# The columns W a of three attention layers: from VectorE to TensorE

## Chip, cores and metric

The kernel runs on one core of a Trainium2 chip. The metric is the device time of one execution in microseconds (us). Each line number below is one of the kernel before.

## What is computed

Four graph attention layers follow one another on x (16 graphs of 1024 nodes with 256 features), all with one 0/1 adjacency matrix. Each layer normalises x per node, applies relu, and adds the layer's result to x. Layers 1 and 3 have 4 heads of 64 columns, layers 2 and 4 one head of 256. In short:

```python
h = relu(layernorm(x))
Wh = h @ W                                   # (N, H * D)
e = leaky(Wh @ a_src + (Wh @ a_dst).T)       # per head, N x N
x = x + act(softmax(where(adj, e, -inf)) @ Wh)   # elu; relu in the last layer
```

Since `Wh @ a = h @ (W @ a)`, the kernel holds for each layer a tile `wx` with the columns of W and, beside them, the columns W a_dst and W a_src of each head. One projection of h by `wx` then gives Wh and both scores. This case is about how the extra columns are made, once per layer.

## The kernel before

**Tiling.** A graph's 1024 nodes lie on 128 partitions as C = 8 blocks, its 256 features as K = 2 halves. Graphs run in four streams, and a step `n` is one layer of one graph; there are 64 steps, in the order that `order_of_steps` writes out (the first steps are layer 1 of graphs 0, 1 and 2, layer 2 of graph 0, and so on).

**A step's work.** A step is prepared while earlier steps are aggregated. VectorE takes statistics (`stats`, L243), GpSimd or VectorE turns them into scale and shift (`combine`, `combine_end`, L272 to L284; all GpSimd in the steps that matter here), ScalarE normalises (L290) and splits the floats into 16-bit halves (L299), a DMA from SyncE's queue transposes them (L301), and ScalarE merges them (L307). TensorE projects (`project`, L332), ScalarE evacuates the result (L334) and takes exponentials (L340, L342), and GpSimd scales (L344). `factors` and `rows` write one row of factors per head to DRAM (L350 to L362), from where SyncE loads it spread over all partitions (`fetch`, L386) and ScalarE copies it to PSUM (`broadcast`, L397). Then VectorE makes the weights, one 128 x 1024 tile for each head and block of neighbours (`weights`, L411, one instruction each). TensorE sums weights times Wh in eight groups per step (`aggregate`, L428): with four heads a group is half a head (64 matmuls, 128 instructions), with one head a block of nodes (8 matmuls, 16 instructions). ScalarE evacuates each group (L443), and `finish` (L464 to L493) divides, applies the activation and adds to x.

**Order.** The program is written out by hand: under `manual_schedule` each engine executes its instructions in the order in which the code issues them. The loop at the end goes through steps and groups; after group k of step n it calls what `later[8 * n + k]` holds, then what `prepare` finds due, then emits more weight tiles.

**Buffers.** The tiles named `w` share 18 slots (`WBUFS`). The weight tiles use them, at first the adjacency rows too, and so do the vectors of `weight_columns`. A tile that finds no free slot waits until an earlier one was read for the last time. PSUM banks named `bank` are four.

**The columns.** `weight_columns(l)` returns four pieces. `vectors` loads a (2 KB) to one partition by one DMA on SyncE's queue (L145). `spread` copies it to all partitions by a matmul with ones (L152) and a ScalarE copy (L155). `columns` makes, for each k and each of the two vectors, a product (L162) and a sum along the row (L163) on VectorE, and the squares of one column set (L169). `bound` sums the squares by TensorE (L175) and derives the layer's constants (L178 to L182). Layer 1 does this at the start. The three other layers do it during the run:

```python
for l, at in ((1, 1), (2, 8 * 3 + 3), (3, 8 * 5 + 3)):
    for i, piece in zip((0, 1, 2, 8), layer[l]):
        later[at + i] = piece
```

So the four pieces follow groups 1, 2, 3 and 9, counted from 0, for the second layer (l = 1), groups 3, 4, 5 and 11 counted from 0 at step 3 for the third (l = 2), and the same from step 5 for the fourth (l = 3).

Of the kernel before, what the change touches and what calls it, by code (L numbers as in the profile page):

```python
# [26 lines left out]
F32 = mybir.dt.float32  # L27
# [4 lines left out]
AF = mybir.ActivationFunctionType  # L32
ALU = mybir.AluOpType
# [3 lines left out]
P = 128  # L37
# [3 lines left out]
WBUFS = 18  # L41
# [29 lines left out]
def kernel(ctx: ExitStack, tc: tile.TileContext, x, adj, ws, avs, out):  # L71
    nc = tc.nc
    B, N, F = x.shape
    C = N // P
    K = F // P
# [4 lines left out]
    ident = const.tile([P, P], F32, name="ident")  # L80
# [10 lines left out]
    wx = []  # L91
# [12 lines left out]
    small = ctx.enter_context(tc.tile_pool(name="small", bufs=4))  # L104
    work = ctx.enter_context(tc.tile_pool(name="work", bufs=2))
# [10 lines left out]
    def bank(*shape):  # L116
        t = ps.tile([P, 512], F32, name="bank")
        n = math.prod(shape)
        if len(shape) == 1:
            return t[:, 0:n]  # L120
        names = "abc"[:len(shape)]
        return t[:, 0:n].rearrange(f"p ({' '.join(names)}) -> p {' '.join(names)}",
                                   **dict(zip(names, shape)))

    def heads_of(t, H):


        return t[..., 0:F + H].rearrange("p c (h d) -> p c h d", h=H)
# [6 lines left out]

    def weight_columns(l):

        H, slope, hs, _ = LAYERS[l]
        D = F // H
        st = {}  # L140

        def vectors(queue=nc.sync):

            st["a"] = work.tile([P, HALF, H, D], F32, name="w", bufs=WBUFS)
            queue.dma_start(  # L145
                out=st["a"][0:1, 2:4],
                in_=bass.AP(tensor=avs[l].tensor, offset=avs[l].offset,
                            ap=[[0, 1], [D, 2], [hs, H], [1, D]]))

        def spread():  # L150
            pa = bank(2, H, D)
            nc.tensor.matmul(pa.rearrange("p t h d -> p (t h d)"), lhsT=ones[0:1, :],  # L152
                             rhs=st["a"][0:1, 2:4].rearrange("p t h d -> p (t h d)"),
                             start=True, stop=True)
            nc.scalar.activation(st["a"][:, 0:2], pa, AF.Copy)  # L155

        def columns(ks=range(K)):
            for k in ks:
                for part in range(2):
                    prod = st["a"][:, 2 + part]  # L160
                    wk = heads_of(wx[l], H)[:, k]
                    nc.vector.tensor_mul(prod, wk[:, :, 0:D], st["a"][:, part])  # L162
                    nc.vector.tensor_reduce(  # L163
                        wk[:, :, D] if part else wx[l][:, k, F + H:F + 2 * H], prod, AX.X, ALU.add)
            if K - 1 not in ks:
                return
            st["sq"] = small.tile([P, K, H], F32, name="sq", bufs=1)
            wd = heads_of(wx[l], H)[:, :, :, D]
            nc.vector.tensor_tensor(st["sq"], wd, wd, op=ALU.mult)  # L169

        def bound():

            pn = bank(H)
            for k in range(K):
                nc.tensor.matmul(pn, lhsT=ones, rhs=st["sq"][:, k, :], start=(k == 0),  # L175
                                 stop=(k == K - 1))
            top = small.tile([P, 1], F32, name="top", bufs=1)
            nc.vector.tensor_reduce(top, pn, AX.X, ALU.max)  # L178
            nc.gpsimd.tensor_tensor(top, top, half1, op=ALU.pow)
            nc.gpsimd.tensor_scalar(cbias[l], top, 16.01, None, op0=ALU.mult)  # L180
            nc.gpsimd.tensor_scalar(nbias[l], top, -16.01 * slope, None, op0=ALU.mult)
            nc.gpsimd.tensor_scalar(rbias[l], top, -16.01 * (1.0 - slope), SHIFT,  # L182
                                    op0=ALU.mult, op1=ALU.add)

        return vectors, spread, columns, bound

    pairs = {}
# [413 lines left out]
    for n, (b, l) in enumerate(steps):  # L601
# [6 lines left out]
        start = 8 * (n - 2)  # L608
# [5 lines left out]
        if free > start + kind[0]:  # L614
            kind = LATE
            start = max(free, agenda_of[-1][0] + 5, start - LATE[7])
        if n == len(steps) - 1:
            kind, start = LAST, 8 * (n - 1)
# [8 lines left out]
    with tc.manual_schedule():  # L627
        blocks = [mask_rows(c) for c in range(C)]
        layer = [weight_columns(l) for l in range(L)]
        layer[0][0](nc.scalar)  # L630
        load(0, 2)
# [100 lines left out]
```

## Time and profile before

| what | value |
|---|---|
| median of 4 runs | 2449.03 us (2447.83 to 2451.18) |
| the profiled execution | 2448.02 us, span 2446.2 us |
| TensorE matmuls busy | 2393.2 us (98% of the span) |
| VectorE busy | 2049.0 us (84%) |
| ScalarE busy | 1478.4 us (60%) |
| GpSimd busy | 1072.7 us (44%) |
| mean granted TensorE clock | 0.996 |
| L162, four layers | 16 instructions, 8.1 us |
| L163, four layers | 16 instructions, 6.7 us |

In the profile PE is TensorE (PEld its weight loads), DVE VectorE, ACT ScalarE, POOL GpSimd and SP SyncE; SPq is SyncE's queue, from which DMAs are issued. A line of the timeline gives the start and the duration in us, engine, line and operation, what is written and read, how many instructions were merged, and in brackets the engine's idle time before it with what ended it. A float32 matmul appears as two instructions. The chain is the sequence of work and waits that ended last, followed back from the end. The granted clock is TensorE's, as a share of full speed.

### The profile page before, as it was taken

The numbers are of one execution on the slowest core, as the hardware profiler recorded it, in microseconds if no ns is written. First come the engines' busy times: TensorE is split into PE (matmuls) and PEld (weight loads), VectorE is DVE, ScalarE is ACT, GpSimd is POOL, SyncE is SP. The second block draws the span as 40 slices with busy tenths as digits, with TensorE's granted clock in tenths as the row PEclk, the third lists the DMA queues.
The fourth block names the chain that finished last, engine by engine and source line by source line (L and its number), as shares of the span: only waits on it lengthen the run. The fifth ranks groups of instructions, "written<-read, shape, count | busy, mean of one in ns | idle before, by whom it ended". The sixth has DMA issues, their size and how long they took to land.

```text
span 2446.2 us, 86561 instructions
## 1 busy us (share of the span) xinstructions
PE 2393.2 (98%) x39127; PEld 2149.3 (88%) x39127; DVE 2049.0 (84%) x2168; ACT 1478.4 (60%) x2499; POOL 1072.7 (44%) x1346
## 2 busy tenths in 40 slices
PE   7999999999999999999999999999999999999999
PEld 5888798889898899898898888999988998988897
DVE  8988688988878988888888889888889888889794
ACT  5464676556665656765556665566665567656542
POOL 3345455443345454544433554543443445554331
PEclk9999999999999999999999999999999999999999
DMA  4322232233333322333333322223324323323310
GB/s 182 81 54 63 44 80 60 73 98 92 101 74 94 80 63 46 80 71 96 107 95 89 80 62 71 63 56 104 83 85 113 97 46 79 69 64 80 71 54 35
DMA packets 290442, 191.84 MB, mean 78 GB/s; under 512 B 259998, under 2 KB 262806, under 8 KB 288152
## 3 DMA queue, kind: packets, MB, share of 16 engines
q1 hardware_dynamic: 290062, 186.29, 30.0%
q8 instruction: 307, 5.03, 0.8%
q14 instruction: 63, 0.52, 0.1%
q10 hardware_dynamic: 10, 0.00, 0.0%
HBM read 104.87 MB, written 17.43 MB: 50 GB/s over the span
## 4 chain that ended last, share of the span: by engine, by line
PE 80%; ACT 7%; DVE 5%; DMA 4%; issue 2%; POOL 1%; SPq 0%; DVEq 0%; ACTq 0%
PE bank L428 62%; PE bank L332 18%; DVE w L411 3%; ACT rows L290 2%; DMA gs<-grow 2%; DMA grow<-gT 2%; ACT rows L299 1%; ACT g L397 1%; ACT rows L481 1%; DMA rows<-rows 1%; ACT y L443 1%; ACT rows L307 1%; DVE bn L243 1%; DVE rows L487 0%; PE bank L358 0%
## 5 line engine op out<-in xcount | busy, mean ns | idle before, releaser
L428 PE MATMUL bank<-whx,w 128*64 128x65 f32 x36864 | 1896.4, 240 | 15.8 <-DVE w L411 9.7
L428 PEld LDWEIGHTS bank<-whx,w 128*64 128x64 f32 x36864 | 1745.5, 144 | 173.1 <-ACT whx L334 21.5
L411 DVE SCALAR_TENSOR_TENSOR w<-g,rcol,mask 128x1024 f32<-128x1024 f32 (+1 forms) x1288 | 1539.6, 1267 | 193.2 <-PE bank L428 162.6
L344 POOL TENSOR_TENSOR whx<-whx 128x1024 f32<-128x1024 f32 x128 | 245.4, 1917 | 840.7 <-ACT whx L342 840.7
L443 ACT ACTIVATE y<-bank 128x260 f32<-128x260 f32 (+1 forms) x504 | 191.7, 381 | 560.5 <-PE bank L428 560.4
L332 PE MATMUL bank<-wx,rows 128*128 128x264 f32 (+1 forms) x2048 | 485.5, 391 | 14.2 <-ACT y L443 6.5
L332 PEld LDWEIGHTS bank<-wx,rows 128*128 128x128 f32 x2048 | 381.4, 191 | 90.1 <-ACT rows L307 12.8
L475 POOL TENSOR_TENSOR y<-y,r 128x1024 f32<-128x1024 f32 x124 | 257.8, 2088 | 224.5 <-DVE rows L474 188.7
L334 ACT ACTIVATE whx<-bank 128x264 f32<-128x264 f32 (+1 forms) x512 | 193.8, 388 | 190.2 <-PE bank L332 189.8
L290 ACT ACTIVATE rows<-x,shift,rstd 128x256 f32<-128x256 f32 x512 | 264.5, 588 | 67.4 <-POOL shift L284 62.3
L488 POOL TENSOR_TENSOR x<-x,rows 128x1024 f32<-128x1024 f32 x94 | 222.3, 2365 | 177.9 <-DVE rows L487 177.9
L307 ACT ACTIVATE rows<-rows 128x2048 uint16<-128x2048 uint16 x122 | 261.7, 2145 | 20.4 <-DMA rows<-rows 20.3
L299 ACT ACTIVATE rows<-rows 128x2048 uint16<-128x2048 uint16 x122 | 233.2, 1911 | 3.9
L487 DVE SCALAR_TENSOR_TENSOR rows<-rows,y 128x1024 f32<-128x1024 f32 x94 | 185.9, 1978 | 45.0 <-ACT rows L481 39.5
L243 DVE BATCH_NORM_STATS2 bn<-x 128x6 f32<-128x256 f32 x512 | 175.8, 410 | 34.4 <-POOL x L488 31.1
L397 ACT ACTIVATE g<-gs 128x1024 f32<-128x1024 f32 x158 | 161.6, 1023 | 63.6 <-DMA gs<-grow 48.7
L278 POOL TENSOR_TENSOR rstd<-rstd,neghalf 128x4 f32<-128x4 f32 (+1 forms) x97 | 121.3, 1251 | 41.1 <-DVE shift L279 33.8
L481 ACT ACTIVATE rows<-rows 128x1024 f32<-128x1024 f32 x96 | 100.6, 1048 | 9.9 <-DVE rows L510 7.9
L464 DVE RECIPROCAL r<-y 128x32 f32<-128x32 f32 (+1 forms) x63 | 17.3, 275 | 98.5 <-ACT y L443 98.5
L474 DVE SCALAR_TENSOR_TENSOR rows<-y,r 128x1024 f32<-128x1024 f32 x58 | 68.5, 1222 | 1.1
L342 ACT ACTIVATE whx<-whx,nbias 128x16 f32<-128x16 f32 (+1 forms) x128 | 40.2, 314 | 4.2
L340 ACT ACTIVATE rcol<-whx,rbias 128x16 f32<-128x16 f32 (+1 forms) x128 | 39.9, 312 | 4.2
(73 smaller groups left out, 465.6 us busy)
## 6 DMA issues: line engine op xcount, KB each, us to landing
gs<-grow SPq DMA_DIRECT2D x158, 512.0 KB
x<-in_x SPq DMA_DIRECT2D x15, 1024.0 KB
out<-x SPq DMA_DIRECT2D x30, 512.0 KB
w<-in_adj SPq DMA_DIRECT2D x8, 512.0 KB
rows<-rows SPq DMA_TRANSPOSE x122
x<-in_x SPq DMA_DIRECT2D x2, 512.0 KB
wx<-in_L_gnn_W SPq DMA_DIRECT2D x8, 128.0 KB
out<-x SPq DMA_DIRECT2D x8, 128.0 KB
```

The lines of the kernel that those rows point to most:

```text
L243: nc.vector.bn_stats(bn[:, c, :], xs[b][:, c, :])
L290: nc.scalar.activation(xn[:, :, q, :], xs[b][:, c, :].rearrange("p (k i) -> p k i", k=K), AF.Relu, bias=st["shift"][:, c:c + 1], scale=st[ ...
L299: nc.scalar.activation(bits, xn.rearrange("p (n s) -> p s n", s=2), AF.Copy)
L307: nc.scalar.activation(st["hT", half].rearrange("p k i -> p (k i)").bitcast(U16).rearrange("p (n s) -> p n s", s=2), st["turned", half].re ...
L332: nc.tensor.matmul(pw, lhsT=st["hT", half][:, k, q * P:(q + 1) * P], rhs=wx[l][:, k, :], start=(k == 0), stop=(k == K - 1))
L334: nc.scalar.activation(st["whx"][:, c, :], pw, AF.Copy)
L344: nc.gpsimd.tensor_tensor(wh[:, :, :, 0:D], wh[:, :, :, 0:D], wh[:, :, :, D:D + 1].to_broadcast([P, HALF, H, D]), op=ALU.mult)
L411: nc.vector.scalar_tensor_tensor(state[n]["w", h, j][:, s], state[n]["g", h][:, s], state[n]["rcol"][:, j, h:h + 1], masks[LAYERS[steps[n] ...
L428: nc.tensor.matmul(acc[o % P:o % P + cols, q, :], lhsT=st["w", h, jc][:, o:o + cols], rhs=st["whx"][:, jc, h * (D + 1):(h + 1) * (D + 1)], ...
L443: nc.scalar.activation(st["y"][:, i0:i0 + per, h, :], acc, AF.Copy)
L475: nc.gpsimd.tensor_tensor(yh, yh, rb, op=ALU.mult)
L488: nc.gpsimd.tensor_add(xh, xh, e)
```

## The change

For the second, third and fourth layer, three of the four pieces are replaced; layer 1 keeps the old ones, `bound` stays, and the places in `later` are the same.

- `vectors_down` lays the vectors down the partitions, one element per partition, in a tile with a column for each vector and head. For four heads the tile is first zeroed on GpSimd, and eight DMAs of 64 elements each follow; for one head there are four DMAs of 128 elements and no zeroing. All are on SyncE's queue.
- `turned` transposes W by matmuls with the identity (four of 128 x 128 for one head, eight of 64 x 128 for four heads) and copies the result to a second tile named `w` on ScalarE.
- `products` multiplies W by the vectors in four small matmuls. Two ScalarE copies bring the columns into `wx`, and GpSimd squares one set.

VectorE no longer takes part in these layers, except for the maximum in `bound`.

```diff
+        def vectors_down():
+            a = st["a"] = work.tile([P, K, 2 * H], F32, name="w", bufs=WBUFS)
+            if H > 1:
+                nc.gpsimd.memset(a, 0.0)
+            for part, column in ((1, 0), (0, H)):
+                for h in range(H):
+                    for k in range(K):
+                        if h * D // P <= k <= ((h + 1) * D - 1) // P:
+                            lo = max(h * D, k * P)
+                            size = min((h + 1) * D, (k + 1) * P) - lo
+                            nc.sync.dma_start(
+                                out=a[lo - k * P:lo - k * P + size, k, column + h:column + h + 1],
+                                in_=bass.AP(tensor=avs[l].tensor,
+                                            offset=avs[l].offset + h * hs + part * D + lo - h * D,
+                                            ap=[[1, size], [1, 1]]))
+        def turned():
+            pt = bank(K, K, P)
+            for k in range(K):
+                wk = heads_of(wx[l], H)[:, k, :, 0:D]
+                size = min(D, P)
+                for lo in range(0, F, size):
+                    h, d = divmod(lo, D)
+                    nc.tensor.matmul(pt[lo % P:lo % P + size, lo // P, k, :],
+                                     lhsT=wk[:, h, d:d + size], rhs=ident, start=True, stop=True)
+            st["wT"] = work.tile([P, K, K, P], F32, name="w", bufs=WBUFS)
+            nc.scalar.activation(st["wT"], pt, AF.Copy)
+        def products():
+            pw = bank(K, 2 * H)
+            for k in range(K):
+                for d in range(K):
+                    nc.tensor.matmul(pw[:, k, :], lhsT=st["wT"][:, d, k, :], rhs=st["a"][:, d, :],
+                                     start=(d == 0), stop=(d == K - 1))
+            wd = heads_of(wx[l], H)[:, :, :, D]
+            nc.scalar.activation(wd, pw[:, :, 0:H], AF.Copy)
+            nc.scalar.activation(wx[l][:, :, F + H:F + 2 * H], pw[:, :, H:2 * H], AF.Copy)
+            st["sq"] = small.tile([P, K, H], F32, name="sq", bufs=1)
+            nc.gpsimd.tensor_tensor(st["sq"], wd, wd, op=ALU.mult)
+        if l > 0:
+            return vectors_down, turned, products, bound
         return vectors, spread, columns, bound
```

## The prediction

> **What bounds the kernel now.** First the page: the busy shares, then the chain that ended last.
>
> ```profile
> PE 2393.2 (98%) x39127; PEld 2149.3 (88%) x39127; DVE 2049.0 (84%) x2168; ACT 1478.4 (60%) x2499; POOL 1072.7 (44%) x1346
> ...
> PE 80%; ACT 7%; DVE 5%; DMA 4%; issue 2%; POOL 1%; SPq 0%; DVEq 0%; ACTq 0%
> ```
>
> TensorE idles 53 of 2446.2 us and carries 80% of the chain, so an edit counts where it lengthens or shortens TensorE's idle time. DVE, which the change relieves, carries 5%. All edits lie before 335 us: the second layer's pieces at 45 to 106 us, the third's at 200 to 240, the fourth's at 283 to 328. What the three places are bound by, the timeline, the chain in order of time and the busy times by stretch must tell.
>
> ```profile
> 62.02 1.12 PE L152 MATMUL bank<-w,ones 1*128 1x512 f32 x2
> ...
> 73.36 26.30 DVE L411 SCALAR_TENSOR_TENSOR w<-g,rcol,mask 128x1024 f32<-128x1024 f32 x22
> ...
> 87.03 3.95 PE L428 MATMUL bank<-whx,w 128*64 128x65 f32 x128
> ...
> 112.14 7.50 PE L428 MATMUL bank<-whx,w 128*64 128x65 f32 x244 [0.86 <-DVE w L411]
> ```
>
> Second layer (timeline): DVE is busy without a gap from 45 to 150 us, and between 109 and 136 TensorE waits for it in nine pieces, some 7 us. Here DVE is the bound.
>
> ```profile
> 200.17 2.79 DMA w<-in_L_gnn_a
> 202.95 0.14 issue
> 203.09 1.09 PE bank L152 x2
> 204.18 10.62 PE bank L428 x48
> 214.80 3.49 PE bank L332 x16
> ...
> 283.74 1.54 DMA w<-in_L_gnn_a
> 285.28 0.14 issue
> 285.41 1.09 PE bank L152 x2
> ```
>
> Third and fourth layer (the chain in order of time): TensorE itself is on the chain, and waits 1.27 and 1.18 us for the vector's DMA before the old spread matmul. A transfer that comes late here is paid in full.
>
> ```profile
> 204.84 0.23 POOL L284 TENSOR_SCALAR shift<-shift 128x4 f32<-128x4 f32 x1
> ...
> 228.97 7.24 DVE L411 SCALAR_TENSOR_TENSOR w<-g,rcol,mask 128x1024 f32<-128x1024 f32 x6 [5.83 <-PE bank L428]
> ```
>
> ```profile
> 249.00:255.00 6.00, 4.74 (x82) 4.55 (x84) 5.99 (x12) 5.97 (x7) 3.31 (x11) 0.50 0.71 137
> ```
>
> For the third layer the timeline adds that GpSimd works on statistics until 205.07, and that DVE later stands 5.8 us for TensorE, so DVE is not the bound there. The row below it is of the busy times by stretch: six microseconds, the busy time and instructions of PE, PEld, DVE, ACT and POOL, then the granted clock, 0.50 after a run of waits.
>
> **Second layer, L162 to L169 gone from DVE.** Nine instructions from 70.02 to 73.36: 3.3 us of the bounding engine. Not all arrives. The 22 products that follow are 1.195 us each; the 17th (it begins at 92.48) is tile 42 in the kernel's count from 0, and needs the slot of tile 24, for there are 18 slots. TensorE last reads tile 24 in the last quarter of the group at 87.03, at about 87.03 + 3.0 + 0.1 = 90.1. TensorE is itself delayed: two small ScalarE copies come ahead of the merge L307, which releases the projection at 71.95; the nearest rows (L340, 0.30) make 0.6. So DVE gains 92.5 - 90.1 - 0.6 = **1.8 us**, which TensorE gets where it waits at 109 to 136. Ends: 3.3 if the slot is free earlier, a loss of 0.6 if DVE turns out not to bind. The vectors' four DMAs (issued from 45.6) have 20 us before they are used; SyncE's next work is at 63.85. The turning (four matmuls, eight instructions; L394 did eight of 128x128 in 1.04) takes the place of the spread (1.12).
>
> **Third layer.** Here the step is moved in the queues, so each is followed.
> - Before, SyncE issued the vector at 200.17. Now the tile is first zeroed on GpSimd, which has both halves' statistics (L272 to L284) ahead in its order, until 205.07. A memset of 128x8 took 0.10, so SyncE starts at 205.2.
> - It then issues eight DMAs of 64 single elements. Back to back, the eight L195 took 4.74, or 0.59 each; the shortest issue rows of SyncE are 0.33, the longest L133 0.69. The last starts seven issues later: 205.2 + 4.1 = 209.3 (207.5 to 210.0). From issue to landing the vector took 1.54 with the rings empty and 2.79 behind a 512 KB load; I take 1.5, as nothing is ahead: **210.8** (209.0 to 212.8).
> - TensorE is free at 201.82 and need not wait for the vectors to turn W: eight logical matmuls, 16 instructions, 1.0 us if column halves overlap as at L428, 2.1 if they do not. The sixth of the step's eight groups follows (10.62 / 3 = 3.54), so it reaches the products at 206.4 to 207.5, say **206.9**, and stands **3.9 us**.
> - The products are eight instructions; L175, four in 0.5 to 0.6, makes 1.1. End 211.9. Before, the same group ended at 204.18 + 3.54 = 207.7. Loss **4.2 us** (2.4 to 6.2).
> - Nothing downstream hides it: the seventh and eighth group, and the projection at 214.64, are TensorE's own chain, and DVE at 228.97 starts when TensorE frees its tiles. The 3.3 us taken from DVE at 208.91 are worth nothing here. With vectors and turned W both held, eight tiles in use and eight ahead fill the 18 slots, so the ninth product ahead must wait until TensorE has done the column products: DVE idles where it did the columns. Behind SyncE's eight issues stands the first transpose (205.72, now about 210); its merge ended 2 us before TensorE's need of 214.64, which itself moves by more than 4. Cost nothing, as the stall covers it; without that cover, some 2 us.
>
> **The clock.** After the waits of 246 to 250 us the granted clock fell to 0.50, and the 228 instructions from 250.75 took 8.83 where 384 at full clock took 11.42: 228 x 0.0297 = 6.8, so 2.0 lost. At 118 to 122 it fell although TensorE was busy 2.30 of 4.00 us, and stayed low for some 6.5. A stall of 3.9 is emptier than either stretch, so I count a fall, with the last two groups under it: 5 us at half rate, **2.5 us** (0 to 3.4). The Trainium skill ("TensorE: Matmul & The Clock Gate", Part 1, the HAM clock gate) has the clock halved after at least one idle window of about 3.4 us and back after one busy window. By that rule a stall of 3.9 would fill a whole window only by luck of phase, and cost about 1.7, an estimate from the page; the row at 118 to 122 speaks for an earlier fall, and the measurement decides.
>
> **Fourth layer.** No memset (one head). Four DMAs in place of one at 283.74; the last lands by 283.74 + 3 x 0.59 + 1.5 = 287.0 (up to 288.6), before the products at 288.9. TensorE saves the wait (1.18), pays turning for spread and 1.1 for the products: about -0.2. But the row of factors (L362, 284.19) and its broadcast (L386) are issued behind, 0.9 to 1.9 us later, and ScalarE's copy of it (L397, 289.07) stands ahead of the evacuations that TensorE's third projection needs; that gives back 0 to 1.5. Together **+0.3** (-1.5 to +1.2). DVE's 4.7 us there lie in idle time: its tiles were ready at 304.5, used at 307.67.
>
> The square on GpSimd, the bound's matmuls L175 and the other copies have tens of microseconds of cover. The Trainium skill ("DMA: Bandwidth & Descriptors", Rules for kernel authors) speaks against the change: a last dimension that isn't contiguous becomes one descriptor per element, to be avoided. No row before shows such a load, so the sum keeps the rows above.
>
> **Sum.** -1.8 + 4.2 + 2.5 + 0.3 = **+5.2 us**. The profiled execution took 2448.02 (span 2446.2 and 1.8 around it), so 2453.2; the median of the runs is 2449.03, 1.0 above, so **2454.2**. The ends: -3.3 + 2.4 + 0 - 1.5 = -2.4, and 0.6 + 6.2 + 3.4 + 1.2 = +11.4.
>
> **Rivals.**
> 1. *The stall stays short of the clock.* Same path, no fall: -1.8 + 2.4 to 4.2 + 0.3, about 2450 to 2452. For it: short waits near 136 and 151 left the clock at 1.00.
> 2. *Not slower: the vectors land before TensorE gets to the products.* It decides at 206.9. Then the third layer is -1.27 - 1.12 + 1.0 + 1.1 = -0.3, the fourth at its best -1.5, and the second up to -3.3: 2444, or 2445.5 with the second at -1.8. Against it: GpSimd ends its statistics at 205.07, which leaves 1.7 us for eight issues and a landing.
> 3. *Element loads are slow to issue.* If each takes a transpose's median on SyncE (1.93), the last starts at 218.7 and lands at 220.2: stall 13, with the clock about +16, or 2465. Against it: every plain SyncE load is 0.26 to 0.69.
>
> That the change does not relieve DVE is no rival; that DVE then waits in place of working is in the sum.
>
> **How the numbers follow.** About 0.2% (4.9 us) is what a measurement of this kernel can tell from no change. The forecast has 0.55, of which its range puts 0.43 above that bound and 0.12 within. Rival 1 has 0.20 (within), rival 2 0.14 (0.09 faster, 0.05 within), rival 3 0.11 (slower). So slower 0.54, within 0.37, faster 0.09. The range 2446.5 to 2460.5 spans the two ends and leaves out rival 3 and the better part of rival 2. The likeliest case alone spans 2452 to 2460.5.
>
> **What would show it.** Right: in the third layer the last vector DMA issues after GpSimd's L284 and TensorE shows a gap of some 4 us on the vectors' DMA ahead of the products, then a clock near 0.50; in the second, TensorE's waits on L411 shrink from 7 to about 5 us; in the fourth, no wait on the vectors. Wrong: products that start at once in the third layer (rival 2), or issue rows above 1 us (rival 3), or time that appears past 335 us, of which this sum has none.

## The result, and the profile after

The changed kernel's median is 2454.74 us (2448.88 to 2463.43), against 2450.63 us of the kernel before, run on the same chips. The ratio is 1.002 with a 95% interval of 1.0014 to 1.0026, which is 3.4 to 6.4 us and at its middle 4.9 us: slower, by about as much as this measurement can tell at all. (The ratio is an estimate of its own and not the quotient of the medians, which are 4.1 us apart.) Two executions on the chip of runs 9 to 11, at 3476.57 and 5638.01 us, were in a slower state and are left out of all ratios and medians below. The profiled execution took 2455.11 us, its span is 2453.3 us.

First the page of the changed kernel: the busy shares and the chain by engine.

```profile
PE 2399.0 (98%) x39177; PEld 2157.9 (88%) x39177; DVE 2038.2 (83%) x2141; ACT 1481.9 (60%) x2505; POOL 1072.5 (44%) x1350
...
PE 85%; ACT 6%; DVE 3%; DMA 3%; issue 2%; POOL 1%; SPq 0%; DVEq 0%; ACTq 0%
```

DVE lost 10.8 us of work, and the span grew by 7.1. TensorE's idle time hardly moved (53.0 before, 2453.3 - 2399.0 = 54.3 now), its busy time grew by 5.8. So the page alone says that no wait took over on the whole, and that TensorE works longer. Both are sums over places that moved in opposite directions; the places have to be read one by one.

A ruler for that is the time at which TensorE starts three projections, in each profile's timeline: one after the second layer's DVE-bound stretch (140.39 us before), one after the third layer's pieces (214.64), one after the fourth's (332.44). What a profile adds between two marks is what that layer cost. A caution: the marks of a kernel are those of one execution, and before 59 us, where TensorE's work is still the same, the executions already differ by -1.4 to +0.3 us; the changed kernel's profile is 0.8 early there (its "early start" below).

| mark | before | after | difference | added by the layer |
|---|---|---|---|---|
| second layer done | 140.39 | 136.59 | -3.80 | -3.0 (0.8 is the early start) |
| third layer done | 214.64 | 220.18 | +5.54 | +9.34 |
| fourth layer done | 332.44 | 338.09 | +5.65 | +0.11 |

**Second layer.** In the timeline (start, duration, engine, line, operation, and in brackets the idle time ahead and what ended it) the kernel before has this at the projection's third block:

```profile
80.64 1.03 ACT L397 ACTIVATE g<-gs 128x1024 f32<-128x1024 f32 x1 [2.32 <-DVE w L411]
82.87 2.13 ACT L307 ACTIVATE rows<-rows 128x2048 uint16<-128x2048 uint16 x1
85.05 2.05 PE L332 MATMUL bank<-wx,rows 128*128 128x264 f32 x8 [1.26 <-ACT rows L307]
```

and the changed kernel this (L455 is the old L411, L441 the old L397, L351 the old L307, L376 the old L332, L472 the old L428):

```profile
48.08 47.75 DVE L455 SCALAR_TENSOR_TENSOR w<-g,rcol,mask 128x1024 f32<-128x1024 f32 x40
...
77.57 1.02 ACT L441 ACTIVATE g<-gs 128x1024 f32<-128x1024 f32 x1
80.27 2.14 ACT L351 ACTIVATE rows<-rows 128x2048 uint16<-128x2048 uint16 x1
83.03 2.05 PE L376 MATMUL bank<-wx,rows 128*128 128x264 f32 x8
...
85.00 3.95 PE L472 MATMUL bank<-whx,w 128*64 128x65 f32 x128
```

Before, ScalarE's copy of the factors waited 2.32 us until DVE had read the previous ones, the merge stood behind that copy, and TensorE behind the merge. With the nine DVE instructions gone, ScalarE no longer waits, nor TensorE, which is here 2.0 us earlier, of which 0.8 is the early start. DVE makes 40 tiles from 48.08 to 95.83 without a gap.

**Third layer.** The timeline of the changed kernel (L328 is the old L284):

```profile
201.02 0.23 POOL L328 TENSOR_SCALAR shift<-shift 128x4 f32<-128x4 f32 x1
201.19 0.11 POOL L190 MEMSET w<- 128x16 f32 x1
201.33 5.55 SPq L197 DMA_DIRECT2D w<-in_L_gnn_a  x8
...
207.64 0.56 PE L219 MATMUL bank<-w 128*128 128x8 f32 x2 [4.92 <-DMA w<-in_L_gnn_a]
208.89 1.42 PE L219 MATMUL bank<-w 128*128 128x8 f32 x6 [0.68 <-DMA w<-in_L_gnn_a]
210.16 10.18 PE L472 MATMUL bank<-whx,w 128*128 128x257 f32 x32
210.50 2.48 DVE L455 SCALAR_TENSOR_TENSOR w<-g,rcol,mask 128x1024 f32<-128x1024 f32 x2 [6.50 <-PE bank L219]
```

The memset follows the last statistics instruction of GpSimd, SyncE's eight issues follow the memset, and TensorE stands 4.92 and 0.68 us for their data. The two groups behind the products take 10.18 us, where three took 10.69 before. The chain in order of time gives the landing of the last vector, and the busy times by stretch (PE, PEld, DVE, ACT, POOL, then the granted clock) the clock over the two groups:

```profile
206.28 2.36 DMA w<-in_L_gnn_a
```

```profile
206.00:216.00 10.00, 7.68 (x22) 6.44 (x23) 2.48 (x2) 3.16 (x5) 0.20 (x1) 0.50 0.57 106
```

**Fourth layer.** Timeline of the changed kernel:

```profile
288.06 2.75 SPq L197 DMA_DIRECT2D w<-in_L_gnn_a  x4
...
290.91 0.29 SPq L406 DMA_DIRECT2D grow<-gT  x1
...
294.11 0.95 PE L219 MATMUL bank<-w 128*128 128x2 f32 x8
...
295.95 1.03 ACT L441 ACTIVATE g<-gs 128x1024 f32<-128x1024 f32 x1 [2.49 <-DMA gs<-grow]
...
297.18 0.17 ACT L222 ACTIVATE wx<-bank 128x2 f32<-128x2 f32 x1
...
297.34 5.61 PE L376 MATMUL bank<-wx,rows 128*128 128x264 f32 x24 [0.40 <-ACT wx L222]
```

No wait for the vectors is left; a small new one stands at the column copy L222, of which more below.

### The profile page after: what moved, and what is told of

The parts are those of the page before. It is cut to its first block, busy times and chain, and to the rows that moved or that the text cites. A ratio compares the mean times of both kernels' runs of the same rounds, so it can differ in the third digit from the quotient of the medians.

```text
span 2453.3 us, 86699 instructions
## 1 busy us (share of the span) xinstructions
PE 2399.0 (98%) x39177; PEld 2157.9 (88%) x39177; DVE 2038.2 (83%) x2141; ACT 1481.9 (60%) x2505; POOL 1072.5 (44%) x1350
## 3 DMA queue, kind: packets, MB, share of 16 engines
q8 instruction: 307, 5.03, 0.8%
## 4 chain that ended last, share of the span: by engine, by line
PE 85%; ACT 6%; DVE 3%; DMA 3%; issue 2%; POOL 1%; SPq 0%; DVEq 0%; ACTq 0%
PE bank L472 66%; PE bank L376 18%; ACT rows L334 2%; DVE w L455 2%; DMA gs<-grow 1%; DMA grow<-gT 1%; ACT rows L343 1%; ACT rows L351 1%; ACT g L441 1%; ACT rows L525 1%; DVE rows L531 1%; DVE bn L287 0%; ACT y L487 0%; DMA rows<-rows 0%; PE bank L402 0%
## 5 line engine op out<-in xcount | busy, mean ns | idle before, releaser
L472 PE MATMUL bank<-whx,w 128*64 128x65 f32 x36864 | 1901.6, 241 | 17.7 <-DVE w L455 8.5
L472 PEld LDWEIGHTS bank<-whx,w 128*64 128x64 f32 x36864 | 1749.3, 144 | 174.4 <-ACT whx L378 22.2
L455 DVE SCALAR_TENSOR_TENSOR w<-g,rcol,mask 128x1024 f32<-128x1024 f32 (+1 forms) x1288 | 1540.0, 1270 | 208.9 <-PE bank L472 168.2
L376 PE MATMUL bank<-wx,rows 128*128 128x264 f32 (+1 forms) x2048 | 484.1, 390 | 11.2 <-ACT y L487 7.2
L376 PEld LDWEIGHTS bank<-wx,rows 128*128 128x128 f32 x2048 | 381.2, 190 | 85.8 <-ACT y L487 11.5
L351 ACT ACTIVATE rows<-rows 128x2048 uint16<-128x2048 uint16 x122 | 261.5, 2144 | 25.2 <-DMA rows<-rows 25.2
L441 ACT ACTIVATE g<-gs 128x1024 f32<-128x1024 f32 x158 | 162.0, 1025 | 58.7 <-DMA gs<-grow 49.7
```

Source lines behind the costliest of these rows:

```text
L351: nc.scalar.activation(st["hT", half].rearrange("p k i -> p (k i)").bitcast(U16).rearrange("p (n s) -> p n s", s=2), st["turned", half].re ...
L376: nc.tensor.matmul(pw, lhsT=st["hT", half][:, k, q * P:(q + 1) * P], rhs=wx[l][:, k, :], start=(k == 0), stop=(k == K - 1))
L455: nc.vector.scalar_tensor_tensor(state[n]["w", h, j][:, s], state[n]["g", h][:, s], state[n]["rcol"][:, j, h:h + 1], masks[LAYERS[steps[n] ...
L472: nc.tensor.matmul(acc[o % P:o % P + cols, q, :], lhsT=st["w", h, jc][:, o:o + cols], rhs=st["whx"][:, jc, h * (D + 1):(h + 1) * (D + 1)], ...
```

## The experiments

What the profile suggests is one theory with two halves: **the second layer gains because DVE, its bound, has less to do; the third loses because its vectors are late (their memset stands behind GpSimd's statistics, and eight issues behind the memset) and because the stall brings the clock down.** The rivals: that the pieces cost TensorE in the third layer by their own work or by holding slots of `w`, whenever the vectors come; that the gain of the second layer is not DVE's; and that something beyond 335 us gives or takes. Each run is given by the three marks and by the time against the kernel before:

| run | second | third | fourth | third layer alone | median against before, us | ratio (95%) |
|---|---|---|---|---|---|---|
| the change | -3.80 | +5.54 | +5.65 | +9.34 | 2454.74 / 2450.63 | 1.0020 (1.0014 to 1.0026) |
| e1_third_only | +0.11 | +8.04 | +7.76 | +7.93 | 2459.23 / 2447.68 | 1.0043 (1.0028 to 1.0057) |
| e2_second_fourth | -3.19 | -1.69 | -1.59 | +1.50 | 2447.58 / 2447.68 | 1.0000 (0.9988 to 1.0013) |
| e3_zero_early | -3.15 | -2.74 | -3.31 | +0.41 | 2449.27 / 2447.68 | 1.0001 (0.9987 to 1.0015) |
| e4_products_later | -3.52 | +0.35 | +0.20 | +3.87 | 2449.34 / 2447.68 | 1.0008 (0.9996 to 1.0020) |
| e5_filled | -3.97 | +1.52 | +1.97 | +5.49 | 2455.33 / 2450.46 | 1.0024 (1.0011 to 1.0038) |
| e6_four_dmas | -4.13 | +2.12 | +2.26 | +6.25 | 2453.99 / 2450.46 | 1.0008 (0.9994 to 1.0022) |
| e7_dve_kept | +0.35 | +8.17 | +7.78 | +7.82 | 2460.77 / 2450.46 | 1.0031 (1.0020 to 1.0042) |
| e8_vectors_early | -3.47 | -3.74 | -3.66 | -0.27 | 2450.71 / 2450.46 | 0.9991 (0.9976 to 1.0005) |
| e9_all_early | -3.74 | -4.00 | -5.06 | -0.26 | 2446.38 / 2450.52 | 0.9987 (0.9974 to 1.0001) |
| e10_early_again | -4.47 | -4.72 | -4.95 | -0.25 | 2447.49 / 2450.52 | 0.9989 (0.9976 to 1.0003) |
| e11_changed_again | -3.96 | +5.32 | +5.45 | +9.28 | 2454.20 / 2450.52 | 1.0018 (1.0006 to 1.0031) |

**1. The third layer alone.** The second and fourth layer keep the old pieces.

```diff
-        if l > 0:
+        if l == 2:
             return vectors_down, turned, products, bound
```

> New pieces for the third layer alone; the second and fourth keep the old ones. Theory (the vectors arrive late and TensorE stands, then runs at the lower clock): all of the loss and none of the gain, +9.3 us against the kernel before (6.2 of stall and 3.1 of clock, as the profile of the changed kernel has them), so about 2460; the projection that began at 214.64 begins at about 224. Rival (the work added to TensorE in each of the three layers makes the loss): a third of it, +1.5 us, and no gap of over 2 us ahead of the products.

The second layer is back at the old time (+0.11), the third costs 7.93 us, and the whole is 1.0043: the third layer alone costs more than the whole change. Timeline of this run (line numbers differ a little from run to run: L197 and the like load the vectors, L219 and the like make the products, L472 and the like aggregate):

```profile
205.22 5.34 SPq L197 DMA_DIRECT2D w<-in_L_gnn_a  x8
...
211.11 0.57 PE L219 MATMUL bank<-w 128*128 128x8 f32 x2 [4.50 <-DMA w<-in_L_gnn_a]
```

The loss is 1.4 us under the expected 9.3: the stall is 0.4 us less, and the clock was down for some 7 us (from 211 to 218) in place of 10. SyncE starts at 205.22, the place that the prediction gave it (205.2) for a second layer that is not early.

**2. The second and fourth layer alone.**

```diff
-        if l > 0:
+        if l in (1, 3):
```

> New pieces for the second and fourth layer, old ones for the third. Theory: the gain without the loss, -3.0 us against the kernel before (second layer -3.0, fourth 0), about 2447.5; the projection that began at 140.39 begins 3 us earlier, and the distance is still 3 us at 332. Rival (work added to TensorE makes the loss): +3 us, two thirds of what the change cost.

The gain of the second layer stands at the first mark (-3.19). In the third layer, which has the old pieces, 1.50 us of it are lost, for a reason that neither the theory nor a rival names:

```profile
199.72 1.09 PE L153 MATMUL bank<-w,ones 1*128 1x512 f32 x2 [1.10 <-DMA w<-in_L_gnn_a]
200.74 12.37 PE L472 MATMUL bank<-whx,w 128*128 128x257 f32 x48
```

The three groups that took 10.69 in the profile before take 12.37: the granted clock averaged 0.60 between 200 and 204 us. The wait ahead is the old one, 1.10 us, which was 1.27 in the kernel before and left the clock at 1.00 there. The time as a whole shows nothing of the 1.6 us that are left at the last mark (1.0000, half an interval being 3 us). What remains is under what the times resolve.

**3. The memset off the path.** The third layer's vectors get a tile of their own, zeroed at the start of the kernel, so that SyncE need not wait for GpSimd.

```diff
+    held = const.tile([P, K, 8], F32, name="held")
+    nc.gpsimd.memset(held, 0.0)
...
-            a = st["a"] = work.tile([P, K, 2 * H], F32, name="w", bufs=WBUFS)
-            if H > 1:
-                nc.gpsimd.memset(a, 0.0)
+            if H > 1:
+                a = st["a"] = held
+            else:
+                a = st["a"] = work.tile([P, K, 2 * H], F32, name="w", bufs=WBUFS)
```

> The changed kernel with the vectors' tile of the third layer held apart from the 18 slots and zeroed at the kernel's start, so that its eight DMAs no longer wait for GpSimd. Theory (GpSimd's order decides when they start): they start when SyncE has issued the loads of factors, 4 us or so before the memset stood, the last lands some 5 us earlier (207.2 on the clock of the profile before, TensorE at the products at 206.4), a stall of about 1 us, no fall of the clock: third layer +1.0 to +1.5 in place of +9.3, the whole about 5 us under before's 2450 plus 3, that is -1.5 to -2 us against the kernel before. Rival (eight issues are too many whenever they start; the landing of single elements is what is slow): the stall shrinks by less than 2 us and the clock still falls, at least +2 us against the kernel before.

```profile
196.91 5.35 SPq L200 DMA_DIRECT2D held<-in_L_gnn_a  x8
...
204.21 0.81 PE L222 MATMUL bank<-held,w 128*128 128x8 f32 x6 [0.56 <-DMA held<-in_L_gnn_a]
204.87 7.20 PE L475 MATMUL bank<-whx,w 128*128 128x257 f32 x32
```

SyncE starts 4.4 us earlier (196.91 against 201.33; 5.1 when the second-layer marks of the two runs, 0.65 apart, are laid on each other), the stall shrinks from 5.60 to 0.56, the clock stays at 1.00, the two groups take 7.20. The third layer costs 0.41 in place of 9.34. So the wait for GpSimd is what makes the vectors late. The vectors' tile no longer takes one of the 18 slots either, but that is not the reason: in the change GpSimd goes from its last statistics instruction (201.02, 0.23 us) to the memset (201.19) without a gap, so the memset waited for no slot. The time as a whole doesn't show the gain of the marks: 1.0001, or -3.2 to +3.7 us, whose lower end is just short of the -3.31 at the last mark. More of this under 8.

**4. The products one group later.** Everything as in the change, but in the third layer the products follow one group later, so that the stall finds cover.

```diff
-    for i, piece in zip((0, 1, 2, 8), layer[l]):
+    for i, piece in zip((0, 1, 3 if l == 2 else 2, 8), layer[l]):
```

> The changed kernel with the column products of the third layer one group later (after the seventh group of its step in place of the sixth), all else alike. Theory: one more group of 3.54 us lies ahead of the wait, so the stall of 5.6 us becomes about 2.1 and the clock stays at 1.00: third layer +2.7 in place of +9.3, in all about -0.3 us against the kernel before. Two theories differ on the clock: if it falls only after a gap of a whole window of some 3.4 us it stays up here; if half a window of idling is enough, as at 118 to 122 us of the profile before, a gap of 2.1 may still bring it down in some executions, and 2 to 3 us more are lost.

Timeline, then the busy times by stretch:

```profile
207.91 0.36 PE L219 MATMUL bank<-w 128*128 128x8 f32 x2 [1.45 <-DMA w<-in_L_gnn_a]
209.08 0.81 PE L219 MATMUL bank<-w 128*128 128x8 f32 x6 [0.82 <-DMA w<-in_L_gnn_a]
```

```profile
210.00:212.00 2.00, 2.00 (x6) 1.54 (x6) 1.92 (x2) 0.26 (x1) 0.00 (x0) 0.50 1.13 211
```

One more group (3.5 us at full clock) covers that much of the stall: 2.27 us remain, and even these brought the clock down for one short while (0.50 at 210 to 212, 0.69 at 212 to 214). The third layer costs 3.87. By the marks this is even with the kernel before (+0.20), and so is the time (1.0008).

**5. The stall filled, the vectors as late as before.** Eleven extra matmuls of identity by W, whose result nobody uses, are issued on TensorE ahead of the products. If the clock's fall comes from idleness, it goes, and the waiting stays.

```diff
+            if l == 2:
+                pd = bank(H, D)
+                for i in range(11):
+                    nc.tensor.matmul(pd, lhsT=ident, rhs=heads_of(wx[l], H)[:, 0, :, 0:D],
+                                     start=True, stop=True)
```

> The changed kernel with eleven more matmuls (the identity by 256 columns, 0.46 us each, their result unused) ahead of the third layer's column products, so that TensorE works through the 5.1 us in which it stood. Theory (the loss there is the wait plus the clock that falls for want of work): the vectors land as before, the wait proper shrinks to under 1 us, the products end within 0.7 us of where they did, but the clock stays at 1.00 and the two groups behind take 7.1 us in place of 9.2 to 10.2: third layer +6.2 in place of +8 to +9.3, 2 to 3 us under the changed kernel. Rival (the clock falls for another reason, such as the small moving matrices of the products): the granted clock is at 0.50 behind the products all the same.

```profile
202.37 4.91 PE L219 MATMUL bank<-wx,ident 128*128 128x256 f32 x22
...
209.12 7.20 PE L477 MATMUL bank<-whx,w 128*128 128x257 f32 x32
```

The clock is 1.00 throughout and the two groups take 7.20 again, 2.98 us less than in the change. The third layer costs 5.49, that is 3.85 less; most of the other 0.9 lies in the products, which took 1.84 from their start to the groups (207.28 to 209.12) in place of 2.52 (207.64 to 210.16). So the loss parts into some 5.5 us of lateness and 3 to 4 us of clock. In the time as a whole the kernel is slower than before (1.0024, 2.7 to 9.3 us); its lower end is near the marks (+1.97, and 0.9 more for an early start), its gain over the change is not resolved.

**6. Half the DMAs, the same elements.** For layers with four heads one DMA per head brings both of its vectors (128 elements), and the products' columns are ordered to fit.

```diff
+            if H > 1:
+                for h in range(H):
+                    k, lo = divmod(h * D, P)
+                    nc.sync.dma_start(
+                        out=a[lo:lo + D, k, h:2 * H:H],
+                        in_=bass.AP(tensor=avs[l].tensor, offset=avs[l].offset + h * hs,
+                                    ap=[[1, D], [D, 2]]))
+                return
...
```

> The changed kernel with the third layer's vectors in four DMAs of 64 x 2 elements (both vectors of a head in one) in place of eight of 64. Theory (each DMA costs SyncE some 0.69 us whatever it holds at this size): four issues take 2.8 us in place of 5.5, the last vector lands 2.7 us earlier, the stall is 2.5 to 3 us in place of 5.6, third layer +3 plus a fall of the clock of 0 to 3. Rival (the cost goes with the number of single elements): the four take as long as the eight did, and nothing changes.

```profile
200.95 3.17 SPq L194 DMA_DIRECT2D w<-in_L_gnn_a  x4
204.63 0.36 PE L227 MATMUL bank<-w 128*128 128x8 f32 x2 [2.26 <-DMA w<-in_L_gnn_a]
```

Four issues take 3.17 us (0.79 each), eight took 5.55 (0.69 each): an issue costs nearly the same with 128 elements as with 64, so the number of DMAs decides. From the last issue to the landing it took 2.35 us, with twice the elements, and 2.36 in the change. The stall is 2.26 and 0.93, 2.4 less than in the change. The clock fell nevertheless, to 0.50 from 206 to 212, and the third layer costs 6.25, just above the expected 3 to 6.

**7. DVE's work kept.** The change whole, and in the second layer nine instructions of the kind taken out are put back on DVE, on tiles that nobody reads.

```diff
+            if l == 1:
+                dead = small.tile([P, H, D], F32, name="dead", bufs=1)
+                dsum = small.tile([P, H], F32, name="dsum", bufs=1)
+                for k in range(K):
+                    wk = heads_of(wx[l], H)[:, k]
+                    for part in range(2):
+                        nc.vector.tensor_mul(dead, wk[:, :, 0:D], wk[:, :, 0:D])
+                        nc.vector.tensor_reduce(dsum, dead, AX.X, ALU.add)
+                nc.vector.tensor_tensor(dsum, dsum, dsum, op=ALU.mult)
```

> The changed kernel with the nine VectorE instructions of the second layer's old columns put back where they stood, on tiles that nothing uses. Theory (the gain in the second layer is VectorE's time, 3.3 us, while VectorE is the bound): the distance to the kernel before at 145 us goes from -3.2 to between 0 and +0.6, the third and fourth layer stay as they are; the whole some 3 us over the changed kernel. Rival (the gain is TensorE's or ScalarE's: no spread, an earlier merge): the distance at 145 us stays at -2 or more.

TensorE's waits between 100 and 140 us (engine, line, who is waited for: sum, times, longest), the first line of the answer for this run, then for the change:

```profile
PE bank L481 <- DVE w L464: 7.0, 9, 0.9
```

```profile
PE bank L472 <- DVE w L455: 5.4, 7, 0.9
```

The waits for DVE are back at what they were (6.6 in the kernel before), and the first mark is at +0.35: nothing is gained where DVE does as much as before, though TensorE, SyncE and ScalarE do what the change has them do. The gain of the second layer is DVE's.

**8. The third layer's vectors early.** As 3, and the vectors are loaded with the second layer's, 150 us ahead of their use.

```diff
+    second, third = later[1], later.pop(27)
+    later[1] = lambda: (second(), third())
```

> The changed kernel with the third layer's vectors loaded at 45 us, right behind the second layer's, into a tile that is held apart and zeroed at the start. Theory: no wait is left in the third layer, neither the new one nor the old one of 1.1 to 1.3 us, and the clock stays up: second layer -3.2, third -0.3, fourth 0, distance to the kernel before -3.5 us at 340 us, about 2445 to 2446 in all; it would beat both kernels, by 0.14%, which is near what the runs can tell. Rival (TensorE's turning and products cost as much as VectorE's relief brings): the distance at 340 us is within 1 us of 0.

```profile
202.95 1.06 PE L222 MATMUL bank<-held,w 128*128 128x8 f32 x8
203.87 7.20 PE L475 MATMUL bank<-whx,w 128*128 128x257 f32 x32
```

No wait ahead of the products, no fall of the clock, and the third layer gains 0.27, as the prediction's second rival had it for vectors that land in time (-0.3). The new work on TensorE is no burden, then. By the marks the kernel is 3.66 us faster than before at 340 us. The time does not show it clearly (0.9991, interval to 1.0005, and the median lies 0.25 us above that of the kernel before). The chain in order of time shows one reason in this execution, 1350 us later:

```profile
1699.98 2.54 issue
```

With two shorter pieces at 1690 and 1695, TensorE waited 4.1 us there for nothing that the profile shows, while DMA's share between 1690 and 1704 was 0.63, and in shorter stretches near 1.0. The kernel before has no such wait there, and run 10, the same kernel as this one, has none either. Other executions have such groups of waits at other places (run 2 between 1168 and 1180 and between 1321 and 1333, run 3 between 1687 and 1699). They come and go with the execution, some 4 us at a time, and hide a gain of 3. What makes them was not tested, but the timeline has a pattern:

```profile
1690.82 0.51 PE L475 MATMUL bank<-whx,w 128*64 128x65 f32 x9 [0.62 <-issue]
1691.26 0.27 PE L405 MATMUL bank<-ident,gcol 128*8 128x128 f32 x1
1691.46 3.65 PE L475 MATMUL bank<-whx,w 128*64 128x65 f32 x117
1696.03 3.95 PE L475 MATMUL bank<-whx,w 128*64 128x65 f32 x128 [0.92 <-issue]
1702.52 0.92 PE L475 MATMUL bank<-whx,w 128*64 128x65 f32 x11 [2.54 <-issue]
```

Between the waits lie 127 and 128 matmuls, with as many weight loads some 256 instructions; in runs 2 and 3 it is 127 or 128 as well. The page of this run counts 39177 matmuls and as many weight loads, and 307 packets on the DMA queue named "instruction" (5.03 MB), which is one packet for 255 of TensorE's instructions. This suggests that TensorE waits there for the next block of its own instructions while other DMAs are busy; it is not shown.

**9 and 10. The fourth layer's vectors early too; and run 8 again.** In 9 the fourth layer's vectors also get a tile of their own and are loaded at the start.

```diff
+    second, third, fourth = later[1], later.pop(27), later.pop(43)
+    later[1] = lambda: (second(), third(), fourth())
...
```

> As the version with early vectors, and the fourth layer's vectors loaded at 45 us too, into another tile held apart: SyncE's row of factors no longer waits behind four issues there. Theory: the distance to the kernel before is -3.6 us at 264 us as with early vectors, and in the fourth layer the saved wait (1.2) and spread (1.1) against turning and products (2.1) and no late factors leave -0.2 to -0.6 more, so -4 at 340 us. The later course, in which single executions differ by up to 10 us, can hide this in the whole time; expected 1 to 4 us under the kernel before. Rival: the fourth layer's late factors cost nothing, and the distance at 340 us is that with early vectors, -3.6.

> The version with early vectors once more, on another day's chip, for the whole time: it was 0.9991 of the kernel before, with an interval from 0.9976 to 1.0005. Theory: -3.5 us at 340 us again, and a ratio between 0.998 and 1.000. Rival (the early gain is given back later in the run): a ratio of 1.000 or more.

Run 9 gains another 1.06 in the fourth layer, where the change had +0.11 and run 10, with the loads in their old place, -0.23. SyncE then issues the row of factors at 279.37 with no loads ahead of it (in run 10 at 280.32, behind four), ScalarE waits 1.02 us for its broadcast in place of 2.49, and TensorE's wait at the column copy (0.38 in run 10) is gone. The times are 0.9987 (to 1.0001) and 0.9989 (to 1.0003), medians 4.1 and 3.0 us below the kernel before. Neither interval of its own leaves out equality. Three on the same side (8, 9 and 10: 2.2 to 3.2 us by the ratios) make a gain likely, but it is not shown, and the median of run 8 does not have it. None of the three intervals reaches up to the changed kernel's ratio.

**11. The change once more, beside 9 and 10.**

> The changed kernel itself beside the two versions with early vectors, on the same chip. Theory: +5.5 us against the kernel before at 340 us of its profile, the whole +4 to +6 us; the versions with early vectors 6 to 9 us under it.

1.0018 (1.0006 to 1.0031), third layer +9.28: the same loss, so the difference between 9 and the change holds on one chip.

## Why the prediction was right, and where its terms were off

The forecast was +5.2 us; the marks show +5.65 at 340 us (6.4 without the early start), the times +4.9. Mechanisms, places and signs were as forecast but for one step, the slot of tile 24; the second layer and the stall were mis-sized, and their errors partly cancel, which was luck. So in part was the absolute figure (2454.2 forecast, 2454.74 measured): the forecast was added to 2449.03, and the kernel before later measured 2450.63.

- **Second layer: -1.8 forecast, -3.0 measured** (3.0 to 3.5 in all the runs with the new pieces and DVE relieved, net of the early start), inside the ends. The step that failed is the slot of tile 24, which was to clip DVE's gain. It held TensorE's time of the last read at 90.1 fixed. But TensorE was itself behind DVE there: ScalarE's copy of the factors waited 2.32 us for DVE and stood ahead of the merge. With DVE relieved the group that reads tile 24 started at 85.00 instead of 87.03, so its slot came free in time, and DVE's 40 tiles from 48.08 on have no gap. TensorE's waits for DVE shrank from 6.6 to 5.4 (eight pieces before, not the nine of the prediction). The 0.6 charged for two small copies was wrong as well: L222, L223 and the merge behind them started at 68.98, 69.03 and 69.09, 0.1 us in all.
- **Third layer, stall: +4.2 forecast, +6.2 measured**, at the upper end. The steps up to SyncE's start held (205.22 in run 1 against 205.2). Mis-sized were the issues, 0.69 each in place of 0.59 (seven of them 4.95 in place of 4.1), and the landing, 2.36 in place of 1.54. The remaining 0.4 is the products', which ended 1.5 after the landing (208.65 to 210.16) in place of 1.1: their last six took 1.42, against 0.81 in run 3 at full clock, so this too is the clock's. For the landing the row taken, one contiguous 2 KB load, misled: loads of single elements took 2.27 to 2.36 in the change and in runs 1 and 3 to 7. Why they take longer was not tested.
- **Clock: +2.5 forecast, +3.1 measured** (10.18 for two groups, against 7.1, two thirds of the 10.69 for three). It was the fall that the prediction read from the row at 118 to 122, only longer: 0.50 for 10 us, where the forecast had some 5 to 6.5. Its size is that of one execution: from the end of the products to the mark the change took 10.0 us, run 11 also 10.0, runs 1 and 7, with a like stall, 9.0 and 8.6, and run 5 without a fall 7.0, so the fall costs 1.6 to 3.0. Run 5 shows that it comes from the idleness, since filling the stall removes it. Rival 1, a stall without the clock, falls with that.
- **Fourth layer: +0.3 forecast, +0.1 measured.** The vectors landed before the products. The row of factors was issued at 290.91, behind four loads; ScalarE's copy of its broadcast (295.95) stood ahead of the column copy L222, and TensorE waited 0.40 for that. The give-back came at the place named, at another copy of the same queue; run 9 gets it back.
- **Nothing downstream hid the stall, and nothing else was late.** The transpose behind the eight issues was merged at 211.52, long before 220.18; DVE stood 6.50 us without anybody waiting for it. Both terms put at zero were zero.
- **Rival 2** (vectors in time) is what run 8 built. By the marks it is 3.7 us faster at 340 us, in the forecast's 3.5 to 5.0 (2445.5 to 2444 against 2449.03), so by them the price was right; the times resolve no gain. The condition was not met: the memset made the vectors late, and the eight issues alone leave a little (run 3, without the memset's wait, still stood 0.56 us). **Rival 3** (slow issues) is out: 0.69, not 1.93.
- The Trainium skill's rule against one descriptor per element ("DMA: Bandwidth & Descriptors", Rules for kernel authors) bore on this case in part only: twice as many elements in a DMA cost little (0.79 against 0.69 to issue, 2.35 against 2.36 to land), the number of DMAs and the place of the memset cost the time.

## What to carry to other kernels

When a step is moved to another queue, price the smallest instruction it brings along: a 0.11 us memset, queued behind statistics of GpSimd, cost 4.4 to 5.1 us of start and with the clock most of the loss. Loads of constants belong where their queue is idle, far ahead of their use, in a tile that the rotating slots don't claim. And follow a "clip" one step back: if the work that seems to clip the gain is itself waiting for the engine that is relieved, it moves along.

## What the hardware showed that was not expected

- The granted clock fell to 0.50 after short waits: 1.10 us in run 2, 1.45 and 0.82 in run 4, 2.26 and 0.93 in run 6. But it stayed at 1.00 after 1.27 us in the kernel before. Falls last about 3.4, 6.8 or 10 us. The Trainium skill ("TensorE: Matmul & The Clock Gate", Part 1, the HAM clock gate) describes a free-running window of about 3.4 us, and the steps of these lengths agree with that; its condition of a whole idle window does not, since no gap in runs 2, 4 and 6 was as long as one. Phase would explain why equal gaps differ between executions; that was only argued.
- A saving of 3 us in the first 340 us of this kernel can't be told in the time of the whole: single executions differ through waits of TensorE that the profile puts to nothing, some 4 us at a time. Marks at the place of the change told what the times could not.
